# Three places instead of five for gathered rows behind the lead-in

## The chip, the core and the metric

The kernel runs on one core of a Trainium2 chip. The metric is device time in microseconds (us) of one launch. A profiled execution gives the trace; other executions, without a profile, give the times.

## What is computed

A graph network layer on 12500 nodes of 256 features and 200000 edges, sorted by their target `dst`:

```python
h = relu(layernorm(x))
agg = segment_sum(h[src], dst)          # 200000 gathered rows of h, added up by target node
z = (1 + eps_gin) * h + agg
t = relu(batchnorm(z @ W1 + b1))        # 256 -> 512, moments over all 12500 nodes
out = x + relu(batchnorm(t @ W2 + b2 + h))
```

Both batch norms need moments over all nodes, so the work falls into three stages: rows and their sums up to `z @ W1`, then the second product, then the last norm and the output. All numbers are float32.

## The kernel before

The 200000 edges are cut into 1563 tiles of 128, and these into 131 groups of `GT` = 12 tiles (the last has three). For every tile, `gather` (L541 to L552) issues one indirect DMA on POOL (GpSimd) that fetches 128 rows of 256 floats, one for each edge. The first `LEAD` = 30 groups gather rows of `x` and normalise them in place (`settle`, L410 to L421), while the same steps compute `h` by chunks of 512 nodes and store it to `h_tab`. From group 30 on rows are gathered from `h_tab`, already normalised.

The step loop has one step per group. The order of instructions on each engine is the written order (`manual_schedule`). Step i issues, in this order: `gather(i + 4)` on POOL (`AHEAD` = 4); additions of finished sums into `zc`, on VectorE (`add`, L679); `take`, which reads one slice of z @ W1 from PSUM for its moments (`bn_stats`, L700), copies it to `ts` (L706) and stores it to `t_tab` on the ACT queue (L707); `spots` (L656) and `hold` (L651), which prepare group i-2 for its placing; `edges(i + 1)` (L583), the one-hot matrices of the next group; and on TensorE (PE) `sums(i)` (L604), 12 accumulating matmuls over the group's tiles, each of which runs as two passes, so that a group has 24. In among these, PE does `put(i - 2)` (L664), which places the sums of an earlier group at their nodes, transposes of `h`, and one slice of the product with W1 (`slice_of`, L689).

Two tiles of every ninth group are not gathered by POOL but fetched row by row on the queues of SP and ACT (`Fetcher`, L475, tiles `one_s` and `one_a`); these groups have ten gathers. SP also loads chunks back into `zc` (L570). The last two groups are summed by `sums_at` (L643), straight at their nodes. At the end of the loop SP loads the first pair of `t_tab` chunks into the two fixed places (L809), which `relu_of` (L427) reads.

Gathered rows lie in a ring of `AHEAD + 1` = 5 places, of 12 tiles each. Three are buffers of a tile pool, `gat`, whose tiles show in the profile as `gt`. Two are fixed, `lands`, each in two pieces: 8 tiles (`gta`) and 4 tiles (`gtb`). The fixed ones exist for the very first groups, whose gathers (L223) are issued before the pool is there. Group i uses place i mod 5: 0 and 1 are the fixed ones, 2 to 4 come from the pool. Within a group tiles are gathered and summed from the last to the first, so a fixed place is written as `gtb` four times, then `gta` eight times. A gather into a pool tile's buffer waits, at the group's first gather, until the group that had it before is summed. A gather into a fixed place waits, at each tile, for the matmul that read that tile before.

The lines that say this:

```python
gat = es.enter_context(tc.tile_pool(name="gat", bufs=AHEAD + 1 - EARLY))     # EARLY = 2
...
k = i % (AHEAD + 1)
ga = early[k] if k < EARLY else ((0, GT, gat.tile([P, GT, D], F32, name="gt")),)
for t in reversed(range(t0, t0 + n)):
```

Of the kernel before, what the change touches and what calls it, by code (L numbers as in the profile page):

```python
# [7 lines left out]
F32 = mybir.dt.float32  # L8
# [7 lines left out]
P = 128  # L16
R = 4
EPS = 1e-5
GT = 12
MARGIN = 64  # L20
AHEAD = 4
LEAD = 30
EARLY = 2
# [15 lines left out]
def kernel(  # L39
# [17 lines left out]
    N, D = x.shape  # L57
# [67 lines left out]
    early = [((0, LOW, a), (LOW, GT, b)) for a, b in lands]  # L125
# [8 lines left out]
    def slot(ga, t):  # L134
        return slots(ga, t)[:, 0, :]
# [205 lines left out]
    def fast():  # L341
# [24 lines left out]
        with ExitStack() as fs:  # L366
# [14 lines left out]
            with ExitStack() as es:  # L381
                ln = es.enter_context(tc.tile_pool(name="ln", bufs=2))
                gat = es.enter_context(tc.tile_pool(name="gat", bufs=AHEAD + 1 - EARLY))
# [109 lines left out]
                def alone(i):  # L493
                    return {f.slots[0]: f for f in (hf, af) if i in f.groups}
# [45 lines left out]
                def gather(i):  # L540
                    t0, n = groups[i]  # L541
                    k = i % (AHEAD + 1)
                    ga = early[k] if k < EARLY else ((0, GT, gat.tile([P, GT, D], F32, name="gt")),)
                    for t in reversed(range(t0, t0 + n)):
                        if t - t0 in alone(i):
                            continue
                        rows = left if t == full_tiles else P
                        nc.gpsimd.indirect_dma_start(  # L548
                            out=slot(ga, t - t0)[:rows], out_offset=None, in_=x if i < LEAD else h_tab,
                            in_offset=bass.IndirectOffsetOnAxis(ap=srcT[:rows, t : t + 1], axis=0),  # L550
                        )
                    gathered[i] = ga  # L552
# [171 lines left out]
                def first(c):  # L724

                    return min(i for i in range(NG) if c in reach(i))
# [6 lines left out]
                for i in range(EARLY, min(AHEAD, NG)):  # L733
                    gather(i)
# [3 lines left out]
                for c in range(NCH):  # L738
                    k = min(max(first(c) + 1, c + 2), NG - CLOSE - 1)
# [4 lines left out]
                for i in range(NG - CLOSE):  # L744
                    before = added
                    gather(i + AHEAD)
                    for k, f in enumerate((hf, af)):
                        if i == hf.begin - 8 + k:
# [54 lines left out]
                for i in range(NG - CLOSE, NG + 1):  # L803
                    if i + AHEAD < NG:
                        gather(i + AHEAD)
# [571 lines left out]
```

## Time and profile before

| | us |
|---|---|
| three runs, median (lowest to highest) | 2539.26 (2533.94 to 2555.35) |
| the profiled execution | 2518.39 |
| its span, first to last instruction | 2516.6 |
| busy: POOL | 1544.2 |
| busy: PE matmuls | 1463.2 |
| busy: VectorE (DVE) | 870.3 |
| busy: ScalarE (ACT) | 404.1 |

A line of a group names code line, engine, operation, the tile written and the tiles read, and the count; then busy time and the mean of one in ns; then the engine's idle time just before these instructions and what ended it. "issue" is a wait for nothing that the profile shows, "remote" one that ended with a signal whose sender the profile does not tell. A line of the timeline has start and length in us, engine, code line, and in brackets the idle time before; neighbours of one kind are merged, with their count. SPq and ACTq are the queues of SP and ACT.

### The profile page before, as it was taken

Reading aid. Unit: us, or ns where it says so; the run is one execution under the profiler, and the core shown is the slowest. Engines: PE = TensorE matmul, PEld = TensorE weight load, DVE = VectorE, ACT = ScalarE, POOL = GpSimd, SP = SyncE. Lnnn points to the kernel's source line nnn. Section 1 sums busy time; section 2 is a strip of 40 time slices with the busy share of each in tenths; the row PEclk is TensorE's granted clock in tenths of the full one; section 3 lists DMA queues with packets and bytes.
Section 4 is the critical chain, followed back from the end, with each engine's and each line's share of the span. In section 5 each row is a group of like instructions: output and inputs, shape, how many; then the busy total and the mean of one; then the engine's idle time right before and its main releaser. Section 6 shows DMA issues by size and latency. Waiting matters only on the chain.

```text
span 2516.6 us, 20994 instructions
## 1 busy us (share of the span) xinstructions
PE 1463.2 (58%) x4856; PEld 1024.8 (41%) x4856; DVE 870.3 (35%) x1360; ACT 404.1 (16%) x755; POOL 1544.2 (61%) x1589
## 2 busy tenths in 40 slices
PE   3265555557455653565375537546446664658997
PEld 2144344435343442443354325324324433446445
DVE  4245445544113221222132213213212321324897
ACT  4265455552000000000000000000000000002554
POOL 7666565566666666655666666665666666662550
PEclk9577778787677876776777767777767767879999
DMA  6365555543334334333343334333333433434988
GB/s 185 117 213 186 173 178 183 161 144 103 108 111 119 109 101 117 111 105 106 95 117 115 104 106 115 108 111 103 105 105 114 118 99 110 114 108 132 319 308 327
DMA packets 150150, 349.86 MB, mean 139 GB/s; under 512 B 32813, under 2 KB 63165, under 8 KB 150015
## 3 DMA queue, kind: packets, MB, share of 16 engines
q0 software_dynamic: 74048, 202.28, 29.0%
q1 hardware_dynamic: 45688, 105.80, 12.3%
q10 hardware_dynamic: 30278, 40.35, 4.5%
q8 instruction: 41, 0.67, 0.1%
q14 instruction: 95, 0.77, 0.1%
HBM read 284.29 MB, written 64.00 MB: 138 GB/s over the span
## 4 chain that ended last, share of the span: by engine, by line
another core or an unknown queue 43%; PE 24%; DVE 16%; issue 10%; ACT 5%; DMA 1%; POOL 1%; ACTq 0%; SPq 0%; DVEq 0%
PE ps L604 11%; DVE oh L583 4%; PE pz L664 3%; PE ph L689 3%; DVE stg L410 3%; ACT gt L421 3%; DVE st L700 2%; PE one L932 2%; DVE zc L679 1%; PE pr L932 1%; DVE ts L706 1%; PE pq L932 1%; DVE at L656 1%; DVE zs L651 1%
## 5 line engine op out<-in xcount | busy, mean ns | idle before, releaser
L548 POOL DMA_INDIRECT gt<-h_tab,srcT x708 | 673.3, 951 | 345.1 <-issue 203.5
L604 PE MATMUL ps<-gt,oh 128*128 128x256 f32 x1824 | 513.0, 427 | 131.2 <-issue 123.1
L664 PE MATMUL pz<-at,zs 128*128 128x256 f32 x516 | 205.9, 536 | 631.5 <-DVE zs L651 286.4
L604 PEld LDWEIGHTS ps<-gt,oh 128*128 128x128 f32 x1824 | 397.9, 219 | 248.0 <-issue 183.3
L700 DVE BATCH_NORM_STATS2 st<-ph 128x6 f32<-128x512 f32 x96 | 67.1, 699 | 1216.2 <-remote 910.3
L664 PEld LDWEIGHTS pz<-at,zs 128*128 128x128 f32 x516 | 124.0, 259 | 701.0 <-issue 449.4
L548 POOL DMA_INDIRECT gta<-h_tab,srcT x315 | 299.6, 951 | 166.0 <-issue 83.4
L604 PE MATMUL ps<-gta,oh 128*128 128x256 f32 x816 | 246.3, 441 | 92.2 <-issue 76.1
L706 ACT COPY ts<-ph 128x512 f32<-128x512 f32 x22 | 12.9, 585 | 1747.2 <-DVE st L700 1721.2
L548 POOL DMA_INDIRECT gt<-in_x_dram,srcT x216 | 204.8, 948 | 120.3 <-issue 75.7
L604 PEld LDWEIGHTS ps<-gta,oh 128*128 128x128 f32 x816 | 185.5, 229 | 150.8 <-issue 111.2
L583 DVE TENSOR_TENSOR oh<-col,dstT 128x1536 f32<-128x1536 f32 x129 | 225.5, 1748 | 0.0
L689 PE MATMUL ph<-zc,w1s 128*128 128x512 f32 (+1 forms) x392 | 194.0, 620 | 34.5 <-DVE hc L534 15.0
L604 PE MATMUL ps<-gtb,oh 128*128 128x256 f32 x416 | 146.6, 461 | 112.2 <-issue 105.1
L548 POOL DMA_INDIRECT gtb<-h_tab,srcT x160 | 151.8, 949 | 97.2 <-remote 54.1
L604 PEld LDWEIGHTS ps<-gtb,oh 128*128 128x128 f32 x416 | 94.4, 231 | 143.3 <-issue 118.0
L679 DVE TENSOR_TENSOR zc<-pz,zc 128x512 f32<-128x512 f32 (+7 forms) x185 | 91.8, 520 | 116.1 <-remote 60.9
L689 PEld LDWEIGHTS ph<-zc,w1s 128*128 128x128 f32 x392 | 76.4, 198 | 101.2 <-issue 71.5
L421 ACT ACTIVATE gt<-gt,nbg,rsg 128x256 f32<-128x256 f32 x216 | 108.2, 587 | 10.0 <-issue 3.8
L548 POOL DMA_INDIRECT gta<-in_x_dram,srcT x80 | 75.8, 948 | 52.1 <-issue 24.2
L651 DVE COPY zs<-ps 128x256 f32<-128x256 f32 x98 | 40.8, 416 | 79.2 <-remote 69.7
L410 DVE BATCH_NORM_STATS2 stg<-gt 128x6 f32<-128x512 f32 x108 | 66.7, 688 | 0.0
(203 smaller groups left out, 1280.3 us busy)
## 6 DMA issues: line engine op xcount, KB each, us to landing
t_tab<-ts ACTq DMA_DIRECT2D x96, 256.0 KB
one_s<-h_tab SPq DMA_DIRECT2D x1280, 1.0 KB
one_a<-h_tab ACTq DMA_DIRECT2D x1280, 1.0 KB
xt<-in_x_dram SPq DMA_DIRECT2D x24, 512.0 KB
h_tab<-ht ACTq DMA_DIRECT2D x24, 512.0 KB
h_cols<-hc SPq DMA_DIRECT2D x24, 512.0 KB
zc<-h_cols SPq DMA_DIRECT2D x24, 512.0 KB
yT<-h_cols SPq DMA_DIRECT2D x24, 512.0 KB
```

The source lines that it names most:

```text
L410: nc.vector.bn_stats(st[:, c : c + 2, :].rearrange("p c s -> p (c s)"), two.rearrange("p c d -> p d c"),)
L421: nc.scalar.activation(slot(to, c), slot(v, c), AF.Relu, bias=nb[:, c : c + 1], scale=rs[:, c : c + 1])
L548: nc.gpsimd.indirect_dma_start(out=slot(ga, t - t0)[:rows], out_offset=None, in_=x if i < LEAD else h_tab, in_offset=bass.IndirectOffsetOn ...
L583: nc.vector.tensor_tensor(ohs[i][:, :n, :], col[:, :P].unsqueeze(1).to_broadcast([P, n, P]), dstT[:, t0 : t0 + n].unsqueeze(2).to_broadcas ...
L604: nc.tensor.matmul(ps, lhsT=oh[:rows, j, :], rhs=fetched[:rows], start=(j == order[0]), stop=(j == order[-1]))
L651: copy(zss[i], summed.pop(i))
L664: nc.tensor.matmul(pz[:, d, :n], lhsT=zs[:, d * P : (d + 1) * P], rhs=at[:, :n], start=True, stop=True)
L679: nc.vector.tensor_add(side, pz[:, :, a - lo : b - lo], side)
L689: nc.tensor.matmul(ph[:, :n], lhsT=w1s[:, d, f * P : (f + 1) * P], rhs=zc[c][:, d, :n], start=(d == 0), stop=(d == DC - 1),)
L700: nc.vector.bn_stats(st1[:, f, c, :], ph[:, :n])
L706: copy(ts[:, :n], ph[:, :n])
L932: nc.tensor.matmul(ps, lhsT=w[:, k, :], rhs=t[:, k, :], start=(k == 0), stop=(k == DC - 1))
```

## The change

From group `LEAD + AHEAD` = 34 on, every group gathers into a tile of the pool, whatever its number. The pool keeps its three buffers. So groups 35 to 130 share three places in turn, group i taking the one that group i-3 had, and the two fixed places are written by no gather after group 31. `gather(i + 4)` is still issued in step i, and nothing else is edited.

```diff
                 def gather(i):
                     t0, n = groups[i]
                     k = i % (AHEAD + 1)
-                    ga = early[k] if k < EARLY else ((0, GT, gat.tile([P, GT, D], F32, name="gt")),)
+                    wide = k < EARLY and i < LEAD + AHEAD
+                    ga = early[k] if wide else ((0, GT, gat.tile([P, GT, D], F32, name="gt")),)
                     for t in reversed(range(t0, t0 + n)):
```

## The prediction

> **What bounds the kernel now.** I read the page first, then the busy times of three stretches: before the first gather that the change moves, from there to the last gather, and the rest.
>
> ```profile
> span 2516.6 us, 20994 instructions
> PE 1463.2 (58%) x4856; PEld 1024.8 (41%) x4856; DVE 870.3 (35%) x1360; ACT 404.1 (16%) x755; POOL 1544.2 (61%) x1589
> ```
> ```profile
> core 0: us, PE busy (x) PEld busy (x) DVE busy (x) ACT busy (x) POOL busy (x), PEclk, DMA share, GB/s
> 0.00:634.00 634.00, 339.31 (x1183) 249.07 (x1184) 289.72 (x532) 289.51 (x599) 401.56 (x432) 0.77 0.54 164
> 634.00:2280.00 1646.00, 909.68 (x2956) 654.91 (x2956) 394.68 (x587) 2.94 (x6) 1067.23 (x1123) 0.74 0.39 109
> 2280.00:2517.00 237.00, 214.21 (x718) 120.87 (x716) 185.90 (x243) 111.61 (x150) 75.38 (x35) 0.98 0.78 278
> ```
>
> The middle stretch holds 1646 of 2517 us, and no engine fills it; POOL, with 1123 gathers, comes nearest. The groups of POOL's instructions in that stretch say what its idle time is:
>
> ```profile
> L548 POOL DMA_INDIRECT gt<-h_tab,srcT x672 | 638.9, 951 | 327.8 <-issue 191.2 <-PE ps L604 70.8 <-remote 60.8
> L548 POOL DMA_INDIRECT gta<-h_tab,srcT x299 | 284.4, 951 | 156.3 <-issue 79.8 <-remote 70.8 <-PE ps L604 5.2
> L548 POOL DMA_INDIRECT gtb<-h_tab,srcT x152 | 144.2, 949 | 94.8 <-remote 53.8 <-issue 35.6 <-PE ps L604 4.8
> ```
>
> A gather is 0.95 us, and 0.30 us of "issue" stand before each in an unbroken run (the timeline below). So 1123 x 1.25 = 1404 us of the 1646 are plain gathering, and 242 us are waits: 327.8 - 672 x 0.30 = 126 in the ring's pool tiles (672 / 12 = 56 groups, 2.25 us each), and 251.1 - 451 x 0.30 = 116 in the two fixed places, `gta` and `gtb` (38 groups, 3.05 us each). That is 2.57 us on each of 94 groups, 15 us of gathering apart. Who ends these waits is PE (L604), which has to give a place free. Why PE is late though it is busy for little more than half of the stretch is seen in the timeline (start, length, engine and line, idle time before):
>
> ```profile
> 1222.74 1.46 PE L604 MATMUL ps<-gtb,oh 128*128 128x256 f32 x6
> 1223.27 14.00 ACTq L475 DMA_DIRECT2D one_a<-h_tab  x7
> ...
> 1228.19 0.95 POOL L548 DMA_INDIRECT gt<-h_tab,srcT  x1 [0.30 <-issue]
> ...
> 1241.97 0.94 POOL L548 DMA_INDIRECT gtb<-h_tab,srcT  x1 [0.30 <-issue]
> ...
> 1253.65 0.95 POOL L548 DMA_INDIRECT gta<-h_tab,srcT  x1 [3.22 <-remote]
> 1256.47 0.95 POOL L548 DMA_INDIRECT gta<-h_tab,srcT  x1 [1.88 <-issue]
> 1258.39 0.70 DVE L700 BATCH_NORM_STATS2 st<-ph 128x6 f32<-128x512 f32 x1 [40.07 <-remote]
> ...
> 1260.54 2.04 PE L664 MATMUL pz<-at,zs 128*128 128x256 f32 x4 [36.34 <-DVE zs L651]
> ```
> ```profile
> 1095.05 9.08 SPq L475 DMA_DIRECT2D one_s<-h_tab  x22
> ```
> ```profile
> 1105.28 0.95 POOL L548 DMA_INDIRECT gt<-h_tab,srcT  x1 [6.44 <-PE ps L604]
> ```
> ```profile
> 1221.88 38.31 SPq L475 DMA_DIRECT2D one_s<-h_tab  x25
> ```
>
> PE stops at 1224.2, three matmul pairs into a group, and waits 36 us for DVE, which itself sat for 40 us before an instruction whose matmul was long over. Meanwhile POOL gathers on without a pause. When POOL is made to wait (3.22, then 1.88 us), everything moves within a few us. SP tells the same: 22 row fetches take 9.08 us (0.41 us each) where POOL mostly stands still (its 6.44 us end at 1105.28), 25 take 38.31 us (1.53 us each) where it runs. So in this trace an unbroken run of gathers holds up the other engines' signals and issues, and a pause of POOL sets them free. The loop feeds on itself: POOL runs until the ring is full, the full ring stops it, the stop lets PE work off groups, and so on. At 1241.97 POOL begins group 70 (its places alternate gtb/gta, gtb/gta, gt, gt, gt) while PE stands in group 66: the ring is full. Counted in this way for groups 38 to 125, four groups are open when POOL begins the next in 69 of 88 cases, three in 12, five in 7. POOL has no lead that it could lose: it leans on the end of the ring, however long the ring is.
>
> **The change part by part.** No instruction is added or removed but one wait of DVE's; PE, ACT, DVE and SP keep their order; 451 gathers change their place. Their price is the same, since both kinds of place show 949 to 951 ns, and so is the price of the matmuls that read them, as their shapes are the same. Each part is one of waits.
>
> (a) *From group 35 on, group i waits for the sums of group i-3, not i-5.* Behind the waiting gather stand only gathers on POOL's queue; who waits for them is PE, three groups later. If POOL and PE keep their times and only the number of the group that POOL works on is moved by two, would PE ever miss a row? The tightest of the groups 36 to 122 is 56, which PE begins at
>
> ```profile
> 1036.68 0.95 POOL L548 DMA_INDIRECT gt<-h_tab,srcT  x1 [0.30 <-issue]
> ...
> 1044.26 1.46 PE L604 MATMUL ps<-gtb,oh 128*128 128x256 f32 x6
> ```
>
> Its third pair of matmuls is at 1045.12; the third gather of group 58, in whose stead group 56 would now be gathered, ends at 1037.63. That leaves 7.5 us for the landing, and more in the 86 others. No row gives the landing; in an unbroken run a gather never waits for the one eight before it, so it is under 8 x 1.25 - 0.95 = 9.1 us. With nothing for it no group is late, with the whole 9.1 four are, by 1.6 us at most, 3 us in all. I take 0, as the old schedule, moved by two groups, can be kept. What is not bounded by this is whether the loop does keep it. From the rows above: if every group waited like those in the pool tiles, 94 x 2.25 = 211 us, 31 less than now; if all waited like those in the fixed places, 94 x 3.05 = 287 us, 45 more. I take the middle, the same 242 us, since PE's need of pauses is what sets them.
>
> (b) *The start.* Group 34 is gathered by 634; group 35 now begins only when group 32 is summed.
>
> ```profile
> 627.85 0.48 PE L604 MATMUL ps<-gt,oh 128*128 128x256 f32 x1 [0.30 <-issue]
> ...
> 634.18 0.95 POOL L548 DMA_INDIRECT gtb<-h_tab,srcT  x1 [0.30 <-issue]
> 634.89 0.58 PE L604 MATMUL ps<-gt,oh 128*128 128x256 f32 x1 [2.21 <-issue]
> ...
> 657.29 4.43 PE L604 MATMUL ps<-gt,oh 128*128 128x256 f32 x10 [0.83 <-issue]
> 657.60 0.95 POOL L548 DMA_INDIRECT gtb<-h_tab,srcT  x1 [4.91 <-remote]
> ...
> 663.74 2.75 PE L604 MATMUL ps<-gt,oh 128*128 128x256 f32 x12
> ```
> ```profile
> 1267.11 1.88 PE L689 MATMUL ph<-zc,w1s 128*128 128x512 f32 x4
> ```
>
> In this trace PE crawls through group 32 (one matmul in 2 to 3 us) until 665.2 (the sixth of the last row's twelve), because POOL runs. Now POOL stands still from 634, so PE gets free after some 3 us (the 3.22 above) and has about 21 matmuls and four of L664 left, 25 x 0.22 = 5.5 us (0.22 is 5.34 / 24 in (c)), and four of L689, 1.9 us: a wait of 10 us. From below 7 (free at once), from above 665.2 - 634.2 = 31 (the crawl stays).
>
> (c) *The end.* The last gathers of now, against PE's last groups:
>
> ```profile
> 2261.83 0.94 POOL L548 DMA_INDIRECT gt<-h_tab,srcT  x1 [3.73 <-remote]
> ...
> 2279.33 0.95 POOL L548 DMA_INDIRECT gta<-h_tab,srcT  x1 [0.30 <-issue]
> ```
> ```profile
> 2278.51 3.62 PE L604 MATMUL ps<-gta,oh 128*128 128x256 f32 x16
> ...
> 2286.12 5.34 PE L604 MATMUL ps<-gt,oh 128*128 128x256 f32 x24
> ...
> 2292.90 5.34 PE L604 MATMUL ps<-gt,oh 128*128 128x256 f32 x24
> ...
> 2307.19 7.48 PE L643 MATMUL ps<-oh,gt 128*128 128x180 f32 x48
> 2314.60 1.72 PE L643 MATMUL pz<-oh,gta 64*128 64x84 f32 x12
> ```
>
> These are groups 126 (over at 2282.1), 127 (2291.5), 128, 129 and 130. Group 129 may now begin at 2282.1 and takes 12 x 1.25 = 15.0 us, to 2297.1; the three gathers of 130 end at 2300.9. PE reads them at 2307.19 and 2314.60, so on PE's clock nothing is late: the z work of L689 and L664 and groups 127 and 128 hide it, with 10 and 13.7 us over. POOL's last gather stands 20.6 us nearer to the end of the kernel than now (2300.9 against 2280.3). From below 0 is saved, if POOL is held up by as much.
>
> (d) *The fixed places are free early.* The four loads of L809 into them need no longer wait for the last groups:
>
> ```profile
> 2261.74 21.76 SPq L809 DMA_DIRECT2D gtb<-t_tab  x2
> ```
> ```profile
> 2319.17 0.81 ACT L427 ACTIVATE gtb<-gtb,of,sc 128x512 f32<-128x512 f32 x1 [0.68 <-DVE of L319]
> ```
>
> What reads them at 2319.17 waits for DVE's constants and not for the load, so this is worth 0.
>
> Sum, on the profiled execution: the gathers end at 2280.3 + 10 (b) + 0 (a) = 2290.3, and 2516.6 - 2300.9 = 215.7 us follow instead of 236.3. Span 2506.0, 10.6 us less; with the 1.8 us around the span 2507.8 against 2518.39. The median of the runs, 2539.26, lies 20.9 us above the profiled execution, so I put the difference on the median: 2529 (0.4% less). The bounds of (a) to (c) together: -31 - 3 from below, +45 + 3 + 21 + 21 from above, which is 2495 to 2619 on the median.
>
> **The rivals.** *Shorter bursts, slower.* After one pause PE at times works off more than three groups: from 1260.54 on it ends 66 and sums 67, 68 and 69, until group 70 begins with this row:
>
> ```profile
> 1298.69 2.52 PE L604 MATMUL ps<-gtb,oh 128*128 128x256 f32 x6
> ```
>
> With three places at most three can lie ready, and PE runs dry where the pause has made it quick. If the bursts lose a quarter of their groups, the pauses grow by a third: 242 / 3 = 81 us, so 2529 + 81 = 2610. It decides from 0.4 us more per group on (38 us, which takes 2529 past 2565, 1% above the median). For it: the tightest spare of 7.5 us, and the long crawls. Against it: the old schedule fits as it stands, and the ring is full in 76 of 88 cases. The Trainium skill, "Perfetto Trace Analysis", Optimization Strategy, has a rule for this side: the same gap repeating on the engine that should be full can mean too little room for the next tile. By it a shorter ring widens POOL's gaps and the time comes out near this rival's; the trace has the repeated gap, but it shows a ring that is full at five.
>
> *Coarser waits, faster.* In the fixed places each gather waits for its own tile's matmul, so a stop comes in the middle of a group, in two or three pieces (3.22, 1.88); in a pool tile only the first gather waits. If the 38 moved groups wait as the 56 others do, 38 x (3.05 - 2.25) = 30 us go: 2499. For it: the three rows of POOL. Against it: PE needs its pauses from somewhere, and a wait that the next group has in its stead saves nothing.
>
> **How the numbers follow.** Within 1% of the median (2514 to 2565, about what a measurement of this kernel can tell from no change) lies my forecast of 2529, with 0.36. The coarser waits, alone or with the gain of the end, give faster by over 1%: 0.30. The shorter bursts give slower by over 1%: 0.34, as a loop that feeds on itself can swing further than its mean says. The likeliest's own range is 2514 to 2565; the range for 8 in 10 reaches to both rivals, 2470 to 2615.
>
> **What would show it.** Right: in the changed kernel's stretch from 634 to the last gather, POOL's idle time beyond 0.30 us per gather is again 2.3 to 2.9 us a group and stands before first gathers of a group alone; two groups are open, not four, when POOL begins the next; the wait before group 35 is some 10 us; from the last gather to the end it is about 216 us. Wrong: idle time of PE before L604 that ends with a gather's landing (now near nothing), POOL's waits above 3 us or below 2.2 us a group, or a last stretch as long as now.

## The result

| | before | changed |
|---|---|---|
| median of four runs (lowest to highest), us | 2547.31 (2533.94 to 2569.66) | 2509.58 (2506.86 to 2513.39) |
| profiled execution, us | 2518.39 | 2506.86 |
| its span, us | 2516.6 | 2505.0 |

The ratio is 0.986, with a 95% interval of 0.983 to 0.990: the change makes the kernel faster by 1.0 to 1.7%. The two profiled executions differ by 11.6 us of span, the medians by 38 us. The profiled execution of before is quicker than the four runs of the table, that of the changed kernel lies 3 us under its median.

The page of the changed kernel, its first two lines, and the three stretches cut where they were cut before (PE, PEld, DVE, ACT, POOL busy, each with its count; then clock, DMA share, GB/s):

```profile
span 2505.0 us, 20581 instructions
PE 1450.5 (58%) x4856; PEld 1018.5 (41%) x4856; DVE 871.1 (35%) x1360; ACT 404.1 (16%) x755; POOL 1542.8 (62%) x1589
```
```profile
0.00:634.00 634.00, 323.72 (x1143) 234.83 (x1144) 288.47 (x530) 290.18 (x599) 396.01 (x426) 0.77 0.53 162
634.00:2280.00 1646.00, 924.19 (x3063) 673.59 (x3061) 404.33 (x602) 4.85 (x10) 1072.74 (x1129) 0.75 0.40 113
2280.00:2505.00 225.00, 202.56 (x652) 110.07 (x652) 178.27 (x229) 109.04 (x146) 74.02 (x34) 0.96 0.77 274
```

No work has gone: the engines have the same counts and nearly the same busy times. The last gathers now end with the middle stretch and 225 us follow them, where 236 did. At the start of the stretch the timeline shows the predicted wait:

```profile
640.53 0.94 POOL L549 DMA_INDIRECT gt<-h_tab,srcT  x1 [0.31 <-issue]
654.13 0.95 POOL L549 DMA_INDIRECT gt<-h_tab,srcT  x1 [12.66 <-PE ps L605]
```

Group 34 ends at 641.5, some 8 us later than before. Its instructions are those of before; in thirteen profiles of before, of the changed kernel and of kernels below that share it (all but the one told of at the end), this end lies between 631 and 647, so this is scatter. Group 35 waits 12.7 us. From there to the end of the last gather it takes 2279.8 - 654.1 = 1625.7 us; before, 2280.3 - 634.2 = 1646.1. So the balance of the span is +7.6 in the lead-in, +12.4 at the start, -20.4 in the middle and -11.1 at the end (236.3 to 225.2), -11.5 in sum. POOL's gathers behind group 34:

```profile
L549 POOL DMA_INDIRECT gt<-h_tab,srcT x1129 | 1072.7, 950 | 573.1 <-issue 323.2 <-remote 193.3 <-PE ps L605 46.0
```

Of the 573.1 us idle, 339 are the 0.30 us before each gather and 12.4 the start; 222 are left, 2.3 us for each of the 95 groups behind group 35, where it was 2.5 to 2.6. All of it stands before first gathers of a group. In 68 of 88 cases two groups are open when POOL begins the next, in 20 one. The waits are much like one another: about 2.5 us after one group gathered without a pause, about 4.5 us after two (medians of 38 and 28 waits).

### The profile page after: what moved, and what is told of

It reads as the page before. It is cut to its first block, busy times and chain, and to the rows that moved or that the text cites. A ratio compares the mean times of both kernels' runs of the same rounds, so it can differ in the third digit from the quotient of the medians.

```text
span 2505.0 us, 20581 instructions
## 1 busy us (share of the span) xinstructions
PE 1450.5 (58%) x4856; PEld 1018.5 (41%) x4856; DVE 871.1 (35%) x1360; ACT 404.1 (16%) x755; POOL 1542.8 (62%) x1589
## 4 chain that ended last, share of the span: by engine, by line
another core or an unknown queue 44%; PE 19%; DVE 18%; issue 11%; ACT 4%; POOL 2%; DMA 1%; SPq 0%; ACTq 0%; DVEq 0%; POOLq 0%
PE ps L605 8%; DVE oh L584 5%; DVE stg L410 3%; PE ph L690 3%; PE pz L665 3%; DVE st L701 2%; PE one L933 2%; DVE zc L680 2%; ACT gt L421 2%; DVE ts L707 1%; PE pr L933 1%; PE pq L933 1%; DVE at L657 1%; POOL gt L549 1%
## 5 line engine op out<-in xcount | busy, mean ns | idle before, releaser
L549 POOL DMA_INDIRECT gt<-h_tab,srcT x1159 | 1101.5, 950 | 590.7 <-issue 331.7
L605 PE MATMUL ps<-gt,oh 128*128 128x256 f32 x2720 | 767.4, 428 | 260.5 <-issue 251.6
L605 PEld LDWEIGHTS ps<-gt,oh 128*128 128x128 f32 x2720 | 594.6, 220 | 427.9 <-issue 321.0
L605 PE MATMUL ps<-gta,oh 128*128 128x256 f32 x224 | 70.7, 452 | 36.5 <-issue 31.3
L605 PEld LDWEIGHTS ps<-gta,oh 128*128 128x128 f32 x224 | 51.4, 234 | 53.6 <-issue 33.8
L605 PE MATMUL ps<-gtb,oh 128*128 128x256 f32 x112 | 42.3, 494 | 40.4 <-issue 19.4
L534 DVE COPY hc<-ph 128x512 f32<-128x512 f32 (+1 forms) x25 | 16.9, 675 | 140.2 <-remote 132.3
L657 DVE TENSOR_SCALAR at<-col,shift 128x256 f32<-128x256 f32 x129 | 61.0, 474 | 0.0
L421 ACT ACTIVATE ht<-xt,nbc,rsc 128x256 f32<-128x256 f32 x98 | 50.9, 589 | 20.3 <-issue 14.5
```

The costliest lines, as they stand in the source:

```text
L421: nc.scalar.activation(slot(to, c), slot(v, c), AF.Relu, bias=nb[:, c : c + 1], scale=rs[:, c : c + 1])
L549: nc.gpsimd.indirect_dma_start(out=slot(ga, t - t0)[:rows], out_offset=None, in_=x if i < LEAD else h_tab, in_offset=bass.IndirectOffsetOn ...
L605: nc.tensor.matmul(ps, lhsT=oh[:rows, j, :], rhs=fetched[:rows], start=(j == order[0]), stop=(j == order[-1]))
L657: nc.vector.tensor_scalar(ats[i][:, :n], col[:, :n], shift[:, i : i + 1], None, op0=OP.is_equal)
```

## The experiments

A common yardstick first: how many gathers POOL gets done in the same 1580 us, from 660 to 2240, in which no engine has anything else to do than this loop. Before and changed kernel (columns as in the stretches above):

```profile
660.00:2240.00 1580.00, 874.54 (x2850) 631.66 (x2849) 379.62 (x563) 0.00 (x0) 1023.37 (x1077) 0.74 0.38 109
```
```profile
660.00:2240.00 1580.00, 876.28 (x2879) 636.43 (x2877) 388.12 (x577) 2.16 (x5) 1035.80 (x1091) 0.75 0.39 112
```

1077 gathers are 1.467 us each, 1091 are 1.448. The question is which part of the change has given these 14 gathers (20 us): the shorter ring, or the way in which its places come free.

**Five places, all released whole.**

```diff
-                    wide = k < EARLY and i < LEAD + AHEAD
+                    wide = k < EARLY
                     ga = early[k] if wide else ((0, GT, gat.tile([P, GT, D], F32, name="gt")),)
-                    for t in reversed(range(t0, t0 + n)):
+                    turned = wide and i >= LEAD + AHEAD
+                    for t in range(t0, t0 + n) if turned else reversed(range(t0, t0 + n)):
```

> Ring of five as before, with the two fixed places still gathered into, but behind the lead-in in the opposite order of tiles, so that a group's first gather waits for the whole group that lay there, as in a pool tile. Release theory (the 20 us that the middle stretch lost come from the way a place is released, whole instead of tile by tile; the length of the ring does nothing): the waits of POOL over groups 36 to 130 fall from 2.51 us a group to about 2.3, as with three places; no wait before group 35; the last stretch stays near 236 us; profiled span about 2517 - 20 = 2497. Ring theory (fewer open groups are what helped): waits 2.5 us a group, span 2517, the median as before. Drain theory (pauses are in proportion to the length of the unbroken run, whoever ends it): pauses stand only between groups, 2.5 us after one group and 4.6 after two, and sum to 2.3 to 2.5 us a group.

Measured: median 2508.76 (2490.26 to 2510.41), ratio 0.986 (0.981 to 0.991), span 2507.8.

```profile
660.00:2240.00 1580.00, 865.73 (x2860) 629.34 (x2859) 381.19 (x567) 0.00 (x0) 1037.05 (x1095) 0.74 0.39 110
```

Five places do what three do, 1095 gathers, and no wait stands before group 35 that is worth naming (2.8 us). The length of the ring is out as a cause. The waits are 2.23 us a group. The middle, from gather 35 to gather 130, is 30 us shorter than before, but what follows the last gather is 249 us, 13 more than before: with four groups open PE still has those to work off. So the span comes to much the same as with three places.

**Three, four and two places in which a tile is written again.** In these three kernels a place is one tile that later groups rewrite. By program order the sums of a group then read what was gathered last into its place, the rows of the group three (three places) or four groups later (two places; in the ring of four at the fixed place alone), so this part of the computation is changed and PE's work on these groups is bound to gathers that come that much later.

```diff
+                    late = i > LEAD + AHEAD
+                    if late and len(held) < 3:
+                        held.append(((0, GT, gat.tile([P, GT, D], F32, name="gt")),))
+                    if late:
+                        ga = held[(i - LEAD - AHEAD - 1) % 3]
```

> Ring of three as in the changed kernel, but each place is one tile that is rewritten, so that every gather waits for the matmul that read its own tile, and a stop can come in the middle of a group. Release theory: all groups wait like those of the fixed places before, 3.05 instead of 2.3 us a group, 94 x 0.75 = 70 us more than the changed kernel, span about 2575. Ring theory: as the changed kernel, span 2505, and waits of 2.3 us a group. Drain theory: the sum of the waits stays at 2.3 to 2.5 us a group but falls into more and shorter pieces; span 2505 to 2525.

Measured: 2534.06 (2517.45 to 2540.90), ratio 0.997 (0.995 to 0.999). In the stretch it makes 1095 gathers, with waits of 2.26 us a group: no sign of the 70 us of the release theory. The time comes from the end: 259 us follow the last gather, as PE stands three groups further back. The same with two places:

```diff
+                    turned = i > LEAD + AHEAD
+                    if turned:
+                        ga = early[(i - LEAD - AHEAD - 1) % 2]
...
+                    for t in range(t0, t0 + n) if turned else reversed(range(t0, t0 + n)):
```

> Ring of two (the two fixed places alone, in the opposite order of tiles, released whole). By the times of before, moved by three groups, 39 of 87 groups would be late, by 179 us in sum; and as PE reads a group's tiles from the last one down while they are now gathered from the first one up, PE has to wait for a whole group besides. If the room of the ring begins to tell below three: span 2505 + 180 = 2685 or more, with idle time of PE before the sums that ends with a gather's landing. If the drain alone sets the pace (a pause of some 2.4 us per group is all that PE needs): within 20 us of the changed kernel, 2485 to 2525.

Measured: 2533.08 (2525.23 to 2546.50), ratio 0.998 (0.994 to 1.002); 1092 gathers, 262 us behind the last. The time lies outside both ranges, and again it is the end that adds to it: the pace is that of the others. And a ring of four, one fixed place and three tiles of the pool:

```diff
+                    if late:
+                        j = (i - LEAD - AHEAD - 1) % 4
+                        turned = j == 0
+                        ga = early[0] if turned else ((0, GT, gat.tile([P, GT, D], F32, name="gt")),)
...
+                    for t in range(t0, t0 + n) if turned else reversed(range(t0, t0 + n)):
```

> Ring of four behind the lead-in, every place released whole (one fixed place in the opposite order of tiles and three pool tiles). Release theory: waits of 2.3 us a group as with three; the wait before group 35 some 3 us instead of 12.7; the last stretch half way between, about 230 us; span about 2500. Ring theory: half way between before and the changed kernel in the middle stretch (10 us off it), span about 2506. Drain theory: as the release theory.

Measured: 2815.14, ratio 1.110 (1.106 to 1.114). The fixed place's sums need a gather four groups ahead, which in its turn waits for the sums of the groups before; POOL and PE go in turns. PE's sums in the 1580 us:

```profile
L611 PE MATMUL ps<-gt,oh 128*128 128x256 f32 x1381 | 326.1, 385 | 6.1 <-issue 6.1
...
L611 PE MATMUL ps<-gtb,oh 128*128 128x256 f32 x152 | 69.3, 608 | 924.0 <-DMA gtb<-h_tab,srcT 924.0
```

So it doesn't tell what a ring of four does, but it shows how a PE looks that waits for rows (924 us that end with a landing), and that its crawl is gone where POOL stands still so often (6.1 us of "issue"). In the changed kernel, from 644 to 2300, it is the other way round:

```profile
L605 PE MATMUL ps<-gt,oh 128*128 128x256 f32 x2288 | 652.4, 432 | 241.5 <-issue 235.4 <-DMA gt<-h_tab,srcT 5.5
```

**The same rings with each group read by its own sums.** Here `gather` of the group that rewrites a place is written behind the sums that read the place. All places are released tile by tile. The cut is that of the ring of five; for three and two, `RING` is 3 and 2, and every place is a new tile of the pool.

```diff
+RING = 5
...
+                    j = i - LEAD - AHEAD - 1
...
+                    else:
+                        if j < RING:
+                            held.append(early[j] if j < EARLY else ((0, GT, gat.tile([P, GT, D], F32, name="gt")),))
+                        ga = held[j % RING]
...
-                    gather(i + AHEAD)
+                    if i <= LEAD:
+                        gather(i + AHEAD)
...
                     sums(i, (puts, turns, slice_ups))
+                    if LEAD + AHEAD < i + RING:
+                        gather(i + RING)
```

> Ring of five behind the lead-in, all five places rewritten tile by tile, so that each gather waits for the one matmul that read its tile (before: three places released whole, two tile by tile). Release theory (a stop in the middle of a group costs more than one between groups): every group waits like those of the fixed places before, 3.05 us, 95 x (3.05 - 2.51) = 51 us more than before, span about 2568. Mixture theory (the two kinds of release in one ring cost, each alone does not): waits of 2.2 to 2.3 us a group, span 2490 to 2510. Drain theory (the pauses are what the gathers need in sum, whoever ends them): 2.2 to 2.5 us a group in many short pieces, span 2490 to 2520.

> Ring of three, each place rewritten tile by tile, with every group's rows read by its own sums (in the run of the three tiles above, the sums of group i read, by program order, the rows of group i+3, so PE's work came three groups later). Release theory: 3.05 us a group against 2.30 in the changed kernel, 70 us more, span about 2575. Mixture and drain theory: 2.2 to 2.3 us a group, span 2500 to 2510 as the changed kernel.

> Ring of two, tile by tile, each group read by its own sums. Room theory (with the times of before moved by three groups 39 of 87 groups are late, by 179 us in sum): idle time of PE before the sums that ends with a landing, span 2505 + 180 = 2685. Drain theory: PE needs 2.2 us of pause per group and has it, the ring gives no more and no less; waits of 2.2 to 2.5 us a group, span 2490 to 2525.

| places, release | ratio to before (95%) | median, us | gathers in the 1580 us | waits per group, us |
|---|---|---|---|---|
| 5, three whole and two by tile (before) | 1 | 2540 to 2547 | 1077 | 2.51 |
| 5, whole | 0.986 (0.981 to 0.991) | 2508.76 | 1095 | 2.23 |
| 5, by tile | 0.988 (0.983 to 0.993) | 2515.15 | 1094 | 2.34 |
| 3, whole (the change) | 0.986 (0.983 to 0.990) | 2509.58 | 1091 | 2.30 |
| 3, by tile | 0.986 (0.982 to 0.991) | 2506.82 | 1090 | 2.34 |
| 2, by tile | 0.984 (0.980 to 0.989) | 2503.55 | 1093 | 2.39 |

The release theory falls (2.34 us by tile, where it had 3.05), the room theory falls (two places are as good as any), and what is left is the mixture. Two kinds of release in one ring cost some 20 us of gathering in the profiled executions, and 26 to 38 us in the medians; either kind alone, with five places or with three, and release by tile with two as well, does not. (A ring of four with one kind of release and each group read by its own sums was not run.) In which stretch the slower runs of before lose the rest, no profile shows. The timeline of before shows the seam between the two kinds:

```profile
1702.54 0.95 POOL L548 DMA_INDIRECT gta<-h_tab,srcT  x1 [2.67 <-remote]
1704.41 2.04 PE L664 MATMUL pz<-at,zs 128*128 128x256 f32 x4 [7.95 <-DVE zs L651]
...
1712.63 2.75 PE L604 MATMUL ps<-gt,oh 128*128 128x256 f32 x12
...
1714.36 0.95 POOL L548 DMA_INDIRECT gt<-h_tab,srcT  x1 [8.37 <-PE ps L604]
```

In the fixed places POOL has come up tile by tile behind PE; the next place is a pool tile, for which PE has to finish a whole further group, and POOL stands for 8.4 us, longer than PE needs to get free. The sum, the number and the longest of the waits of pool tiles that the profile puts down to PE's sums, before and changed (the view of waits, same stretch; those marked "remote" reach 4.5 us before and 5.0 in the changed kernel):

```profile
POOL gt L548 <- PE ps L604: 70.8, 18, 8.4
```
```profile
POOL gt L549 <- PE ps L605: 33.0, 12, 3.0
```

By place, over 19 groups each, the waits of before are 3.2 and 2.9 us a group in the two fixed places, 3.3 in the first pool tile behind them, 1.6 and 1.7 in the other two; in the changed kernel they are 2.2 to 2.5 in each place. So the seam shows in the mean, but it is not all: the fixed places too wait longer than in the ring of five by tile (2.2 to 2.5 at every place), and why they do is not shown.

**A mixed ring of three.** The ring of three by tile, with one place turned into a whole one:

```diff
-                    for t in reversed(range(t0, t0 + n)):
+                    whole = j >= 0 and j % RING == 0
+                    for t in range(t0, t0 + n) if whole else reversed(range(t0, t0 + n)):
```

> Ring of three in which the two kinds of release are mixed, as in the ring of five before: one place is gathered in the opposite order of tiles, so that its group's first gather waits for the whole group there, the other two are released tile by tile. Mixture theory (the change from tile by tile to whole costs: POOL has come to PE's heels tile by tile, and must then wait for a whole group): waits of 2.5 us a group or more against 2.34 in the ring of three tiles, over 2 us of them at the whole places, and a median some 20 us above it, 2525. Drain theory alone (the gathers need their pauses in sum, whoever ends them): 2.3 us a group, median 2507.

Measured: 2572.81 (2567.95 to 2578.54), ratio 1.010 (1.005 to 1.016), slower than before and 66 us above the unmixed ring.

```profile
660.00:2240.00 1580.00, 858.76 (x2762) 616.87 (x2761) 368.34 (x546) 0.00 (x0) 999.22 (x1051) 0.73 0.38 108
```
```profile
POOL gt L558 <- PE ps L614: 117.3, 35, 10.8
```

1051 gathers, 3.01 us of waits a group; before the first gather of the whole place 3.9 us on the mean, up to 10.8. The place gathered just before it, by tile, has 4.4 us in sum, the one behind it 0.8. The direction is the mixture theory's, the size three times its own. But another thing may have a share: at the whole place the tile that PE reads first is gathered last, and PE waits for landings, 45 us from 644 to 2300 against the 5.5 of the changed kernel.

```profile
L614 PE MATMUL ps<-gt,oh 128*128 128x256 f32 x2193 | 643.7, 440 | 280.0 <-issue 234.0 <-DMA gt<-h_tab,srcT 45.4
```

The control was to be the same ring with all three places turned:

```diff
-                    whole = j >= 0 and j % RING == 0
+                    whole = j >= 0
```

> Control to the mixed ring of three: all three places are gathered in the opposite order of tiles, so that each is released whole and none tile by tile; the tile that PE reads first lands last at every place, where in the mixed ring it did so at one place of three. Mixture theory: no mixing, so waits of 2.3 us a group and a median near the 2507 of the two pure rings of three, at most 20 us above it for rows that land late. Order theory (the mixed ring was slow because the tile that PE needs first came last: 45 us of PE's idle time there ended with a landing): three places do it instead of one, so at least as slow as the mixed ring, 2573 or more, with over 45 us of PE's idle time ending with a landing.

Measured: 2154.52 against a before of 2146.65 in the same series of runs, ratio 1.004 (1.003 to 1.005). In this series the kernel before itself took 15% less than in all others, so the run says nothing on the mixture; what it shows instead is told at the end. How much of the 66 us is the order of tiles stays open. In the ring of five the mixture was undone from both sides, by whole release with two turned places and by tile with none, and both gave the same.

**POOL without anything to wait for.** The last question is why 2.2 to 2.4 us of waits per group come back in every unmixed ring.

```diff
+                    if late:
+                        ga = held[(i - LEAD - AHEAD - 1) % 3]
...
-                    gathered[i] = ga
+                    gathered[i] = early[i % 2] if late else ga
```

> From group 35 on the gathers go into three tiles that nobody reads, and the sums read rows gathered long before instead of their own (this part of the computation is left out), so POOL waits for nobody and PE for no gather. Hold-up theory (an unbroken run of gathers holds up the other engines, and only a pause of POOL sets them free): POOL runs 1129 gathers in 1129 x 1.25 = 1411 us, to about 2050; in that time PE goes on crawling at 0.1 to 0.3 matmul per us as it does 24 us into a run now, and does at most 420 of its 3060 matmuls of this stretch; it does the rest afterwards, which puts the span at 3000 or more. Rival (PE is held by its own chain with DVE and by its clock, and POOL merely waits for its places): PE keeps 17 us a group or does better, and the span is 2300 to 2510.

Measured: 3014.53 us, span 3012.7. The stretches, two while POOL gathers and one when it has ended:

```profile
1000.00:1500.00 500.00, 85.10 (x188) 49.95 (x188) 25.40 (x38) 0.00 (x0) 389.77 (x359) 0.53 0.34 98
1500.00:2050.00 550.00, 88.67 (x184) 50.09 (x184) 24.30 (x36) 0.00 (x0) 429.19 (x393) 0.52 0.34 97
2300.00:2800.00 500.00, 495.15 (x2062) 392.56 (x2061) 270.24 (x408) 5.82 (x12) 0.00 (x0) 0.99 0.15 50
```

With POOL gathering PE does a third of a matmul per us; with POOL silent 4.1, busy for 495 of 500 us. PE reads no row here that was gathered from group 35 on, so it isn't for POOL's rows that it waits. Its crawl has a beat (PEld is PE's loading of weights):

```profile
1476.32 0.59 PE L612 MATMUL ps<-gta,oh 128*128 128x256 f32 x1 [1.73 <-issue]
...
1477.72 0.29 PEld L612 LDWEIGHTS ps<-gta,oh 128*128 128x128 f32 x1 [2.61 <-issue]
...
1479.12 0.58 PE L612 MATMUL ps<-gta,oh 128*128 128x256 f32 x1 [2.21 <-issue]
...
1480.52 0.29 PEld L612 LDWEIGHTS ps<-gtb,oh 128*128 128x128 f32 x1 [2.51 <-issue]
...
1481.92 0.59 PE L612 MATMUL ps<-gtb,oh 128*128 128x256 f32 x1 [2.21 <-issue]
```

One matmul in 2.80 us, with a load of weights midway: one step in 1.40 us. And POOL itself did not keep its 1.25 us a gather, as I had expected it to. From 700 to 860, and from 1000 to 2000:

```profile
L556 POOL DMA_INDIRECT gt<-h_tab,srcT x128 | 121.0, 946 | 39.0 <-issue 39.0
```
```profile
L556 POOL DMA_INDIRECT gt<-h_tab,srcT x715 | 781.2, 1093 | 220.2 <-issue 220.2
```

160 / 128 = 1.25 us a gather at first; 174 gathers after the last pause it becomes 1.40 (1093 ns and 0.30), and stays so until the end at 2201.7 (not 2050). PE's beat is older than that. It begins 15 us after POOL's last pause, when POOL still issues a gather per 1.25 us, and the kernel of before has it in its loop, beside gathers at 1.25 us:

```profile
1341.12 0.95 POOL L548 DMA_INDIRECT gta<-h_tab,srcT  x1 [0.30 <-issue]
...
1342.37 0.95 POOL L548 DMA_INDIRECT gta<-h_tab,srcT  x1 [0.31 <-issue]
1342.80 0.59 PE L604 MATMUL ps<-gt,oh 128*128 128x256 f32 x1 [2.21 <-issue]
...
1344.20 0.29 PEld L604 LDWEIGHTS ps<-gt,oh 128*128 128x128 f32 x1 [2.51 <-issue]
...
1345.60 0.59 PE L604 MATMUL ps<-gt,oh 128*128 128x256 f32 x1 [2.21 <-issue]
```

So beside an unbroken run of gathers something lets PE make one step in 1.40 us, and POOL itself comes under the same 1.40 us only late. The transfers of the gathers are not what lags. While PE crawls and POOL still issues at 1.25 us, bytes move at 108 GB/s, against 97 to 98 afterwards, 10% less for a step that is 12% longer:

```profile
710.00:900.00 190.00, 32.67 (x62) 16.51 (x61) 4.97 (x7) 0.00 (x0) 143.68 (x152) 0.52 0.38 108
```

The DMA packets of the trace say the same (queue q0, where 16 packets of 4 bytes close each gather): a gather's last packet ends 2.4 us after the gather's start up to the 174th gather, and 2.6 us after it from there on (medians), so no transfers pile up behind POOL. What moves on once in 1.40 us the runs don't show. If POOL runs ahead of it by 0.15 us with each gather, that is 1.8 us in a group of 12, and the waits of 2.2 to 2.4 us a group would be this difference and 0.5 us more. This is a sum that comes near, and not a cause that is shown.

**Half the bytes.** The same kernel, with rows of 512 bytes:

```diff
-                            out=slot(ga, t - t0)[:rows], out_offset=None, in_=x if i < LEAD else h_tab,
+                            out=slot(ga, t - t0)[:rows, : D // 2] if late else slot(ga, t - t0)[:rows],
+                            out_offset=None,
+                            in_=x if i < LEAD else h_tab.rearrange("n (k d) -> (n k) d", k=2) if late else h_tab,
```

> As the run with the unread gathers, but each of them fetches rows of 512 bytes instead of 1024 (128 of them as before; nobody reads them, and the sums read rows gathered long before). Drain by rows (the 1.40 us per gather at which the long run settled is the price of 128 row descriptors): the long run settles at 1.40 us again, PE crawls until it ends near 2200, span about 3010. Drain by bytes: 0.70 us a gather, which is under the 1.25 us at which POOL issues them, so nothing piles up: POOL stays at 1.25 us a gather and ends near 2051, PE does its 3060 matmuls at some 4 per us beside it and is done before POOL, and the span is about 2050 + 215 = 2270. Rival to both (the issue of gathers itself holds up the other engines, piled up or not): POOL at 1.25 us throughout and PE still crawling, span near 2850.

Measured: 3010.69 us. From 1000 to 2000, and the stretch from 1500:

```profile
L556 POOL DMA_INDIRECT gt<-h_tab,srcT x714 | 776.3, 1087 | 224.6 <-issue 224.6
```
```profile
1500.00:2050.00 550.00, 88.50 (x184) 49.98 (x184) 24.75 (x37) 0.00 (x0) 426.69 (x394) 0.52 0.20 50
```

The rate of bytes halves, from 97 to 50 GB/s, and all else stays, the 1.40 us with it: the price does not go by bytes. Whether it goes by rows or by gathers is open, as no run has gathers of fewer rows. The rival of the issue itself isn't met by this run, since POOL came to 1.40 us here too; what speaks against it is the series told of at the end, where POOL issues at 1.25 us and PE doesn't crawl.

**A rest that waits for nobody.**

```diff
+                        if t == t0 + GT // 2 and LEAD + AHEAD < i < NG - CLOSE:
+                            rest = lands[0][1][:, :3, :]
+                            nc.gpsimd.tensor_add(rest, rest, rest)
```

> The changed kernel with an addition of 128 x 768 on POOL in the middle of each group from 35 to 125 (1.8 us and 0.3 of issue, by the 2.36 us that 128 x 1024 take in the last stretch), a rest that waits for nobody. A group of 12 gathers and a rest takes 15.0 + 2.1 = 17.1 us, 1.42 us a gather, just above the 1.40 us at which the long run of unread gathers settled. Drain theory: the rest takes the place of the waits, which fall from 2.3 to under 0.5 us a group; the middle stretch stays within 15 us of now, the median 2495 to 2520. If the waits are PE's own need (it must be given 2.3 us before it ends a group) the rest comes on top: 91 x 2.1 = 191 us more, 2700.

Measured: 2522.00 (2513.44 to 2522.74), ratio 0.989 (0.984 to 0.995). POOL in the same 1580 us:

```profile
L552 POOL DMA_INDIRECT gt<-h_tab,srcT x1086 | 1031.3, 950 | 428.6 <-issue 304.1 <-remote 95.0 <-PE ps L608 27.2
L548 POOL TENSOR_TENSOR gtb<-gtb 128x768 f32<-128x768 f32 x91 | 134.4, 1477 | 1.5
```

The changed kernel has 1580 - 1091 x 1.25 = 216 us of waits in this stretch. Here 1580 - 1086 x 1.25 = 222 us are not gathering: some 120 us of rests (1.48 us each, not 1.8) and some 100 us of waits, 1.12 us a group. So the rests took the place of as much waiting. Two things that I expected missed: 1.12 us of waits a group are left, not under 0.5, and the median lies 2 us above its range. From the first gather of group 35 to the last it takes 1636 us, 10 more than in the changed kernel. To within these 10 us a pause is worth the same whoever makes it: the loop needs some 2.3 us of POOL's silence per group, and why so much is open.

## Why the prediction was right, and where it was wrong

The forecast of 2529 lies 19 us above the median and the range held it; the measurement tells the ratio from 1, so it is the case "faster by over 1%" that came, to which I gave 0.30, and not the likeliest one. The profiled span came out at 2505.0 where the sum had 2506.0. That is luck: the middle was 20 us shorter than forecast, the lead-in 8 us longer by scatter, the wait before group 35 some 2 us longer and the end 9.5 us longer, and these errors cancel.

**The loop.** That an unbroken run of gathers holds up the other engines, and that the full ring is what stops it, stands, and is now shown: PE goes at a twelfth of its pace beside a POOL that never stops, though it needs nothing of POOL's. What I didn't see is the beat of 1.40 us, and that POOL itself falls to it in a long run. What the waits are worth is bounded by the unread gathers: with nothing to wait for they take 1547 us from group 35 on, against 1626 in the changed kernel, and PE pays for it.

**(a), the step that failed.** I bounded it by the waits of the two kinds of place, -31 to +45, and took the middle, "the same 242 us". It was -20, and -30 with five whole places, the lower end. The two kinds were not two prices: five places by tile have 2.34 us, not 3.05. The 3.05 goes with standing next to places of the other kind. The rows by tile name that I took for prices of each kind were measured in a mixture and hold only there. That the old schedule fits when moved by two groups was right (the landing that I could bound only by 9.1 us is 2.4 us, the median of before's DMA packets), and for three groups it was of no use: by it two places should have had 39 late groups and 179 us, and PE's idle time before its sums that ends with a landing is 11 us there, because PE's times move with POOL's.

**(b)** 10 us predicted, 12.7 measured, within the bounds.

**(c), mis-sized.** 215.7 us behind the last gather were predicted, 225.2 measured, and of 20.6 us gained there are 11.1. The bound was named ("if POOL is held up by as much") but the held-up side is PE:

```profile
2278.90 0.94 POOL L549 DMA_INDIRECT gt<-h_tab,srcT  x1 [0.30 <-issue]
```
```profile
2283.32 2.08 PE L665 MATMUL pz<-at,zs 128*128 128x256 f32 x4 [6.71 <-ACT zs L652]
2285.78 8.94 PE L690 MATMUL ph<-zc,w1s 128*128 128x512 f32 x16 [0.38 <-DVE zc L680]
2294.56 7.48 PE L644 MATMUL ps<-oh,gt 128*128 128x180 f32 x48
...
2308.13 7.13 PE L962 MATMUL pq<-gtb,w2s 128*128 128x512 f32 x16 [1.12 <-ACT gtb L427]
```

The last two groups are gathered in one run, ACT's copy comes late out of it, and PE begins its last placings only when POOL has ended. I had let PE keep its clock of before. From L962 on both kernels take the same 197 us. **(d)** was worth nothing, as predicted.

**The median.** I put the difference of the profiled executions on the median. That step failed most: 12 us of span, but 38 us of medians. The profile of before was of its quickest run. How far each kernel's runs scatter I hadn't asked: 19 runs of before in one series reach from 2522.55 to 2561.89, the four of the changed kernel from 2506.86 to 2513.39. That mixing is what makes them scatter is not shown, as the four runs of five whole places span 20 us too.

**The rivals.** "Coarser waits" (2499) had the right part of the change, the fixed places, and nearly the right size for the middle, for a wrong reason: waits by tile are no dearer, mixed ones are. "Shorter bursts" (2610) did not come: PE's idle time before its sums that ends with a landing is 5.5 us, against 13.5 before. For the rule of the Trainium skill, "Perfetto Trace Analysis", Optimization Strategy, on the repeated gap as want of room, the runs answer that here it isn't: rings of five, three and two whose places are alike repeat the same gap.

**What would show it.** All four signs came: 2.3 us a group before first gathers alone, two open groups, a wait before group 35 (12.7), and a shorter end (225, not 216).

## What to carry to other kernels

Look whether the places of one ring come free in the same way: tile by tile beside whole cost 1.2 to 1.6% here, the number of places (five, three or two) nothing that could be told. Where a producer that nothing stops holds up the engines that must free its places, as the gathers do here, its waits come back whatever the buffers; letting it run without anything to wait for shows this, and its packets show whether the transfers are what lags. And a difference of two profiled executions goes on the median only after one has seen how either kernel's runs scatter.

## What the runs showed of the hardware

Gathers of 128 rows by an indirect DMA are issued at 1.25 us; in an unbroken run POOL falls to 1.40 us a gather, after 174 gathers of 1024-byte rows and after 169 of 512-byte rows. Beside such a run PE makes one step (a load of weights or a matmul) in 1.40 us, from 10 to 12 gathers after a pause on, while a gather's last packet still ends 2.2 to 2.6 us behind its start.

One series of the runs did not show this at all. There the kernel before took 2146.65 us (2143.89 to 2148.82, nine runs) at a granted clock of 0.87 to 0.88, where it was 0.76 to 0.77 in the others, and the ring of three with all places turned:

```profile
L558 POOL DMA_INDIRECT gt<-h_tab,srcT x1070 | 1015.9, 949 | 326.3 <-issue 324.1 <-DMA gt<-h_tab,srcT 1.2 <-PE ps L614 0.9
```
```profile
L614 PE MATMUL ps<-gt,oh 128*128 128x256 f32 x2138 | 634.5, 451 | 461.2 <-DMA gt<-h_tab,srcT 444.7 <-DVE oh L593 16.6
```

From 600 to the last gather POOL goes on at 1.25 us a gather with no wait in 1070 of them, PE has no "issue" time left, and its idle time ends with landings: POOL's issue is the bound, and neither ring nor release can matter to it. The gathers land 2.4 us after their start there too, so it is the crawl that is missing and not a faster transfer. Why, the runs don't show; it isn't another chip, as the record has the same one for the series with the rings by tile, where the kernel before took 2541.64 us. Nor do they show whether the change is worth anything there, as the changed kernel wasn't run in that series.
